# The gated tokens' product with wo: inside the recurrence's loop, or behind its last state

## The chip, the cores and the metric

The kernel runs on one core of a Trainium2 chip. The metric is the device time of one execution in microseconds (us). The kernel before took 2483.61 us (median of three runs, 2482.64 to 2483.89). One further execution was recorded by the hardware profiler; its trace is what this document reads.

Engines are named as in the profile: PE is TensorE's matmuls, PEld its weight loads, DVE is VectorE, ACT is ScalarE, POOL is GpSimd, SP is SyncE, which here only issues DMAs.

## The reference

The program is two layers over x of 32 sequences of 128 tokens, 512 wide. The first layer and the second layer's routed experts come earlier in the kernel and are not touched. The change lies in the last part, a recurrence over the 32 sequences followed by an output product:

```python
# z = r * y: the gated tokens, from the part before (32 x 128 x 512)
def step(c, xt):
    ft = sigmoid(xt @ wf.T + c @ uf.T + bf)
    it = sigmoid(xt @ wi.T + c @ ui.T + bi)
    gt = tanh(xt @ wc.T + c @ uc.T + bc)
    c = ft * c + it * gt
    return (c, None)
c_final, _ = lax.scan(step, c0, z)
h = tanh(einsum('tbi,oi->tbo', z, wo) + c_final @ uo.T + bo)
x = x1 + h
```

Two things matter. The steps of the scan depend on one another through the state c, which is 128 x 512. The product of z with wo does not depend on c at all; only the final sum does, which needs the last state.

## The kernel before

**Number format.** Every matmul with fp32 accuracy is made of three: both operands are split into a high and a low half (`split`, L64 on ACT for the high half, L65 on DVE for the low one), and `mm3` (L82) multiplies high by high, high by low and low by high for each of KD = 4 slices of the contraction. So one product of 128 x 512 by 512 x 512 is 12 matmuls of 512 columns. A weight pair takes 16 KB of each partition.

**Tiling.** A block b is one of NB = 32 steps of the scan (128 rows, one for each position in a sequence). Four blocks make a group: NG = 8 groups of GT = 512 rows. z of a group is held as `zs[g]`, a pair of halves in pool `zp`, which has two buffers.

**The loop** (from L1677 on) runs over t = 0 to 31. One step is, in the order of the program: three products of the state, `from_c` for c, i and f, each followed by its gate (`gate`: addition of the bias on DVE from PSUM, sigmoid or tanh on ACT); the new state (`new_c`, two DVE operations); the products of the next step's input, `from_x`, for c and i; four transposes of the new state (`turn`, tile ptC) and the split of the result, cT; `from_x` for f; then `gate_y` for block t+2. `gate_y` takes r through a sigmoid on ACT and multiplies it by y on DVE, transposes the product on PE (tile ptF, one PSUM bank) and splits it from PSUM into `zs[g]`. `get_y` then asks for r (a load on SP's queue) and y (an indirect gather on POOL's queue) two blocks ahead; both have two buffers.

The step ends with `unit(t - 2)`. A unit is one of 32 pieces of the product of z with wo: n is divided into the group g and the slice o of 128 output columns, and a unit is 12 matmuls into a PSUM bank poF. There are two banks for it (`ps_z`). For groups 0 to 4 ACT copies the result to `zo` and its own queue stores it to DRAM (`zo_d`); for groups 5 and 6 it stays on chip (`zok`); group 7's four results stay in PSUM. Groups are only complete once their fourth block is gated, so unit n is taken in step n + 2, and the last four (group 7) in steps 30 and 31 and behind them.

At t = 29 the input weights are no longer needed. Their memory (pool `wx_p`) is given to a pool `op`, and loads of stored results and of x1 begin (`load_groups`, `load_part`). Other pieces go into memory that other tiles leave free: the recurrent weights' pools `uci` and `uf_p`, the biases' tiles, staging tiles.

**Behind the last state**: `cu`, the product of the state with uo, 48 matmuls of 128 columns, into four PSUM banks; then `to_z`, which adds the same product, broadcast over the group's four blocks, to group 7's banks with 48 matmuls of 512 columns. Each of the 32 results then takes an addition of cu (DVE, L1768; not for group 7), a tanh with the bias bo1 (ACT, L1774), an addition of x1 on DVE and POOL by turns (L1777), and a store of 256 KB on SP's queue (L1778).

**Order.** The program's order gives the priority, but the framework places instructions for each engine ahead of time. Something that it expects to be ready can be placed ahead of something that is written earlier. At t = 31, 13 matmuls of units stand ahead of the transposes of the last state, though they are written behind them. [...]`issue_after` keeps a block of instructions behind a given one.

Of the kernel before, what the change touches and what calls it, by code (L numbers as in the profile page):

```python
# [20 lines left out]
P = 128  # L21
D = 512
KD = D // P
NB = 32
# [25 lines left out]
def tile_kernel(ctx: ExitStack, tc: tile.TileContext, a: dict, out: bass.AP):  # L50
# [40 lines left out]
    hid_d = [dram.tile([n, P, KD * P], F32, tag=f"hid{i}", name=f"hid_d{i}") for i, n in enumerate(PARTS)]  # L91
    xh_d = [dram.tile([n, P, KD * P], F32, tag=f"xh{i}", name=f"xh_d{i}") for i, n in enumerate(PARTS)]
    x1_d = dram.tile([NB, P, KD, P], F32, tag="x1", name="x1_d")
    zo_d = [dram.tile([P, KD, GT], F32, tag=f"zo{g}", name=f"zo_d{g}") for g in range(NG)]
    bias_d = dram.tile([E0 * P, 3 * KD], F32, tag="bias", name="bias_d")

    v_d = dram.tile([N, D], F32, tag="v", name="v_d")
# [1416 lines left out]

    with sf:
        kw = dict(reuse_waits="tile")
        ZS = 2

        zop = sf.enter_context(tc.tile_pool(name="zop", bufs=4, side="right", **kw))
        uf_p = sf.enter_context(tc.tile_pool(name="uf_p", bufs=1, side="right", **kw))  # L1520
# [33 lines left out]
        def gate_y(b):  # L1554
            g, j = divmod(b, GB)
            y, r = ys.pop(b)
            if b >= LEAD:
                nc.scalar.activation(r, r, AF.Sigmoid)
            nc.vector.tensor_tensor(r, y, r, ALU.mult)  # L1559
            if j == 0:  # L1560
                zs[g] = zp.tile([P, 2, KD, GT], FR, tag="z", name=f"z_{g}")
            pt = ps_y.tile([P, KD, P], F32, tag="t", name=f"ptF_{b}")
            for k in range(KD):
                nc.tensor.transpose(pt[:, k, :], r[:, bass.ts(k, P)], ident)  # L1564
            s = bass.ts(j, P)
            return split(zs[g][:, 0, :, s], zs[g][:, 1, :, s], pt)

        def turn(c, t):
            pt = ps_c.tile([P, KD, P], F32, tag="t", name=f"ptC_{t}")
# [29 lines left out]
            nc.vector.tensor_tensor(new, v["f"], v["i"], ALU.add)  # L1599
            return new  # L1600

        pos, zos, x1s = {}, {}, {}

        def unit(n, k0=0, k1=KD):

            if n < 0:
                return
            g, o = divmod(n, KD)
            last = g == NG - 1
            if k0 == 0:  # L1610
                pool, tag = ((ps_z, "z"), (ps_z, "z"), (ps_y, "t"), (ps_g, "g"))[o if last else 0]
                pos[o] = pool.tile([P, GT], F32, tag=tag, name=f"poF_{g}_{o}")
            po = pos[o]
            mm3(
                po, lambda h, k: wo1[:, h, k0 + k, bass.ts(o, P)],
                lambda h, k: zs[g][:, h, k0 + k, :], k1 - k0, k0 == 0, not last,
            )
            if last:
                pass
            elif g >= NG - 1 - ZS:  # L1620
                if o % 2 == 0:
                    zok = zop.tile([P, 2, GT], F32, tag="raw", name=f"zok_{g}_{o}")
                    zos[g, o], zos[g, o + 1] = zok[:, 0, :], zok[:, 1, :]
                nc.scalar.copy(zos[g, o], po)
            else:
                zo = yp.tile([P, GT], F32, tag="zo", name=f"zo_{g}_{o}")
                nc.scalar.copy(zo, po)
                nc.scalar.dma_start(out=zo_d[g][:, o, :], in_=zo)

        def load_groups(pool, tag, todo):  # L1630

            t = pool.tile([P, len(todo), KD, GT], F32, tag=tag, name="in_" + "_".join(f"{d}{g}" for d, g in todo))
            for n, (d, g) in enumerate(todo):
                if d == "x":
                    by = t[:, n].rearrange("p o q -> p (o q)").rearrange("p (b o q) -> p b o q", b=GB, q=P)
                    nc.sync.dma_start(
                        out=by.rearrange("p b o q -> p b (o q)"),
                        in_=x1_d[g * GB : (g + 1) * GB].rearrange("b p o q -> p b (o q)"),
                    )
                    for o in range(KD):  # L1640
                        x1s[g, o] = by[:, :, o, :]
                    continue
                nc.sync.dma_start(out=t[:, n], in_=zo_d[g])
                for o in range(KD):
                    zos[g, o] = t[:, n, o, :]

        def load_part(pool, tag, d, g, o, parts=1):
            t = pool.tile([P, parts, GT], F32, tag=tag, name=f"in_{d}{g}_{o}")
            if d == "x":
                for n in range(parts):  # L1650
                    x1s[g, o + n] = by = t[:, n, :].rearrange("p (b q) -> p b q", q=P)
                    nc.sync.dma_start(
                        out=by, in_=x1_d[g * GB : (g + 1) * GB, :, o + n, :].rearrange("b p q -> p b q")
                    )
                return
            nc.sync.dma_start(out=t, in_=zo_d[g][:, o : o + parts, :])
            for n in range(parts):
                zos[g, o + n] = t[:, n, :]

        ps, wx = {}, {}  # L1660

# [19 lines left out]
        for t in range(NB):  # L1681
            cT = cT_next
            v = {}
            if t == 0:
                done = from_x(0, ps, "ci", False, True)
                with tc.issue_after(done):
                    from_x(0, ps, "f", False, True)
                with tc.issue_after(z_done):
                    wo1 = weight("wo", keep_p, yp, 2, "zo", KD)
                for n in "cif":  # L1690
                    gate(t, n, ps, v, bias)
            elif t < NB - 1:
                for n in "cif":
                    late = from_c(t, n, ps, cT, False, True)
                    gate(t, n, ps, v, bias)
            else:
                for n in "cif":
                    from_c(t, n, ps, cT, True, True)
                    gate(t, n, ps, v, stash)
# [14 lines left out]
            for b in ((t + LEAD,) if t < NB - 4 else (NB - 2, NB - 1) if t == NB - 4 else ()):  # L1714
                gate_y(b)
                if b + LEAD < NB:
                    get_y(b + LEAD)
            for n in (t - 2,) if t < NB - 2 else (NB - 4, NB - 3) if t == NB - 2 else (NB - 2,):
                unit(n)
            if t == NB - 3:  # L1720
                sx.close()
                op = sf.enter_context(tc.tile_pool(name="op", bufs=1, side="right", **kw))
                load_groups(op, "a", [("x", 7), ("x", 6)])
                load_groups(op, "b", [("x", 5), ("x", 0)])
                load_groups(zp, "z", [("z", 0), ("x", 1)])
                uo1 = op.tile([P, 2, KD, D], FR, tag="uo", name="uo_hl")
                for k in range(KD):
                    raw = yp.tile([P, D], F32, tag="yr"[k % 2], name=f"raw_uo{k}")
                    nc.sync.dma_start(out=raw, in_=a["uo"][:, k, :])
                    split(uo1[:, 0, k], uo1[:, 1, k], raw)  # L1730
                with tc.issue_after(late):
                    load_part(first_p, "c0", "x", 3, 0)
                    load_part(first_p, "cT0", "x", 3, 1, 2)
                load_part(yp, "zo", "x", 3, 3)
                load_part(yp, "zo", "z", 2, 3)
            if t == NB - 2:
                for o, n in enumerate("cif"):
                    load_part(keep_p, "b" + n, "z", 2, o)
        load_groups(uci, "uc", [("z", 3), ("x", 4)])
        load_groups(uci, "ui", [("z", 4), ("z", 1)])  # L1740
        load_groups(uf_p, "uf", [("x", 2)])

        cT = cT_next
        unit(NB - 1, 0, KD // 2)
        cu = []
        for o in range(KD):
            pool, tag = (ps_c, "t") if o == 0 else (ps_g, "g")
            cu.append(pool.tile([P, P], F32, tag=tag, name=f"cu_{o}"))
            mm3(cu[o], lambda h, k: uo1[:, h, k, bass.ts(o, P)], lambda h, k: cT[:, h, k, :], KD)

        def to_z(o):
            mm3(
                pos[o], lambda h, k: uo1[:, h, k, bass.ts(o, P)],
                lambda h, k: cT[:, h, k, :].unsqueeze(1).to_broadcast([P, GB, P]), KD, False, True,
            )

        unit(NB - 1, KD // 2, KD)
        units = [(g, o) for g in (6, 5, 0, 1, 2, 3, 4) for o in range(KD)]
        for o in range(KD):
            units.insert(3 + 5 * o, (NG - 1, o))  # L1760
        for n, (g, o) in enumerate(units):
            if g == NG - 1:
                to_z(o)
                src = pos.pop(o)
                h = yp.tile([P, GT], F32, tag="y", name=f"hF_{g}_{o}")
            else:
                src = h = zos[g, o]
                nc.vector.tensor_tensor(  # L1768
                    h.rearrange("p (b t) -> p b t", t=P),
                    h.rearrange("p (b t) -> p b t", t=P),  # L1770
                    cu[o].unsqueeze(1).to_broadcast([P, GB, P]),
                    ALU.add,
                )
            nc.scalar.activation(h, src, AF.Tanh, bias=bo1[:, o : o + 1])  # L1774
            x1 = x1s[g, o]
            by = h.rearrange("p (b q) -> p b q", q=P)
            (nc.gpsimd if n % 2 else nc.vector).tensor_tensor(by, by, x1, ALU.add)  # L1777
            nc.sync.dma_start(out=out[g][:, o, :], in_=h)  # L1778


# [86 lines left out]
```

## Time and profile before

| | us |
|---|---|
| median of three runs | 2483.61 |
| the profiled execution's own time | 2483.24 |
| its span, first to last instruction | 2481.50 |
| first recurrent product (ps_c of t = 0) starts | 1796.07 |
| last matmul ends | 2459.82 |

| from 1796.07 to 2459.82 (663.75 us) | busy us |
|---|---|
| PE | 660.79 |
| DVE | 225.21 |
| ACT | 153.06 |
| POOL | 44.07 |

The trace gives each instruction's start and duration. Matmuls are pipelined, so a row of 12 shows a little more than twelve times their spacing; the spacing is read from the starts of successive rows. A name such as `poF<-z,wo_hl` is the tile that is written and those that are read. In a list of waits, the row names the engine and tile that waited, the one it waited for, the total in us, how often, and the longest. The granted clock is the share of TensorE's full clock that the chip allowed. In rows of DMAs, the last figure is the median time from issue to landing.

### The profile page before, as it was taken

What the parts mean: (1) busy time and instruction counts of PE and PEld (TensorE: products, weight loads), DVE (VectorE), ACT (ScalarE), POOL (GpSimd) and SP (SyncE); (2) the same over time, 40 slices, a digit from 0 to 9 for tenths busy, and PEclk for the clock granted to TensorE, in tenths of its full rate; (3) what the DMA queues carried; (4) which work ended last, traced back from release to release, by engine and by line L of the source; (5) the groups of instructions that cost most, each with busy time, mean ns of one, the idle gap of its engine ahead of it and who ended that gap; (6) DMA issues with size and microseconds to landing.
All of it is one profiled execution on the core that took longest, in us unless ns stands there. A gap on an engine that the chain in (4) does not pass through costs nothing.

```text
span 2481.5 us, 36586 instructions
## 1 busy us (share of the span) xinstructions
PE 2429.9 (98%) x12918; PEld 2057.4 (83%) x12918; DVE 1331.9 (54%) x2283; ACT 1035.4 (42%) x1826; POOL 410.5 (17%) x462
## 2 busy tenths in 40 slices
PE   8999999999999999999999999999999999999996
PEld 6788888888887888888888799999878888888885
DVE  8796654556567454365454586676643333333326
ACT  5545533443223644454554476666522222222214
POOL 1000022222232333322232100000010000000003
PEclk9999999999999999999999999999999999999998
DMA  6545555556564253342342577777431111111027
GB/s 211 150 126 175 187 172 165 187 183 228 172 211 149 95 160 114 103 154 69 104 161 87 189 262 236 227 222 231 166 110 39 42 40 43 43 39 39 26 72 280
DMA packets 193404, 351.63 MB, mean 142 GB/s; under 512 B 37504, under 2 KB 72368, under 8 KB 190144
## 3 DMA queue, kind: packets, MB, share of 16 engines
q1 hardware_dynamic: 141792, 245.99, 29.9%
q0 software_dynamic: 36448, 75.95, 10.3%
q10 hardware_dynamic: 14976, 27.27, 3.0%
q8 instruction: 108, 1.77, 0.3%
q14 instruction: 80, 0.66, 0.1%
HBM read 373.94 MB, written 88.65 MB: 186 GB/s over the span
## 4 chain that ended last, share of the span: by engine, by line
PE 52%; DVE 1%; DMA 1%; ACT 0%; issue 0%; POOL 0%; POOLq 0%; DVEq 0%; ACTq 0%
PE phD L82 7%; PE ps_c L82 7%; PE ps_f L82 7%; PE ps_i L82 7%; PE poD L82 7%; PE poF L82 3%; PE po L82 3%; PE pb L82 2%; PE pv L82 2%; PE ptF L1564 1%; PE ptC L1571 1%; PE ptD L1431 1%; PE ptB L1256 0%; PE pr L1176 0%; DMA rowsD<-xk_d,slot_t 0%
## 5 line engine op out<-in xcount | busy, mean ns | idle before, releaser
L65 DVE TENSOR_TENSOR wD<-rawD,wD 128x1024 fp32r<-128x1024 f32 x128 | 156.5, 1229 | 82.1 <-ACT wD L64 82.1
L82 PE MATMUL p<-xhl,swu 128*128 128x512 f32 x768 | 190.4, 399 | 6.2 <-ACT xhl L64 6.2
L82 PE MATMUL p<-xhl,kept_u 128*128 128x512 f32 x768 | 185.9, 397 | 0.7 <-DVE kept_u L65 0.7
L82 PEld LDWEIGHTS phD<-xe,wD 128*128 128x128 f32 x1536 | 184.3, 189 | 2.1 <-ACT xe L64 0.9
L82 PE MATMUL phD<-xe,wD 128*128 128x256 f32 x1536 | 185.0, 280 | 0.7 <-ACT xe L64 0.7
L82 PE MATMUL poD<-wD,hD 128*128 128x512 f32 x768 | 181.6, 392 | 0.0
L82 PEld LDWEIGHTS p<-xhl,swu 128*128 128x128 f32 x768 | 145.7, 192 | 36.8 <-ACT xhl L64 6.2
L82 PEld LDWEIGHTS p<-xhl,kept_u 128*128 128x128 f32 x768 | 143.0, 189 | 30.4 <-DVE kept_u L65 1.1
L82 PEld LDWEIGHTS poD<-wD,hD 128*128 128x128 f32 x768 | 141.9, 188 | 28.3
L64 ACT CAST wD<-rawD 128x1024 fp32r<-128x1024 f32 x128 | 133.3, 1046 | 56.1 <-PE poD L82 54.1
L290 POOL DMA_INDIRECT xg<-in_x_rows_dram,blk_t x71 | 67.7, 954 | 442.6 <-PE ptx L300 242.9
L1536 POOL DMA_INDIRECT y<-res_d,gat_i x32 | 30.5, 952 | 573.8 <-DVE r L1559 492.9
L82 PE MATMUL pur<-r,xb 128*128 x792 | 110.3, 288 | 3.2 <-issue 1.2
L82 PE MATMUL por<-r,hbr 128*128 x396 | 107.9, 407 | 1.2 <-ACT hbr L64 1.1
L65 DVE TENSOR_TENSOR xb<-ptx,xb 128x512 fp32r<-128x512 f32 x68 | 47.0, 691 | 105.7 <-ACT xb L64 103.9
L82 PEld LDWEIGHTS pur<-r,xb 128*128 128x128 f32 x792 | 98.3, 189 | 5.3 <-issue 1.8
L82 PE MATMUL poF<-z,wo_hl 128*128 128x512 f32 x384 | 96.4, 399 | 0.0
L82 PE MATMUL ps_f<-wf_hl,z 128*128 128x512 f32 x384 | 96.2, 399 | 0.0
L82 PE MATMUL pb<-rT,Wo_hl 128*128 128x256 f32 x768 | 95.2, 281 | 0.3 <-DVE rT L65 0.2
L82 PE MATMUL ps_c<-wc_hl,z 128*128 128x512 f32 x384 | 94.7, 396 | 0.7 <-ACT z L64 0.7
L82 PE MATMUL pv<-w_recept_hl,xr 128*128 128x512 f32 x384 | 94.2, 395 | 0.0
L82 PE MATMUL acc<-swd,as 128*128 128x512 f32 x384 | 93.5, 390 | 0.0
(1031 smaller groups left out, 4950.1 us busy)
## 6 DMA issues: line engine op xcount, KB each, us to landing
rawD<-in_w_key_dram SPq DMA_DIRECT2D x64, 512.0 KB, 4.2
rawD<-in_w_value_dram SPq DMA_DIRECT2D x64, 512.0 KB, 4.2
swr<-in_sw_dram SPq DMA_DIRECT2D x120, 256.0 KB, 3.3
o_d<-obr SPq DMA_DIRECT2D x66, 256.0 KB, 2.3
rraw<-in_rw_dram SPq DMA_DIRECT2D x32, 256.0 KB, 3.0
xc<-in_x_dram SPq DMA_DIRECT2D x32, 256.0 KB, 3.6
hid_d<-o ACTq DMA_DIRECT2D x32, 256.0 KB, 2.3
xh_d<-xc SPq DMA_DIRECT2D x32, 256.0 KB, 2.9
```

What stands on the lines that cost most here:

```text
L64: first = nc.scalar.copy(hi, src).ins
L65: done = nc.vector.tensor_tensor(lo, src, hi.bitcast(F32), ALU.subtract).ins
L82: done = nc.tensor.matmul(ps, lhsT=left(hl, k), rhs=right(hr, k), start=start and k + n == 0, stop=stop and 3 * k + n == last,)
L290: nc.gpsimd.indirect_dma_start(out=xg[i], out_offset=None, in_=a["x_rows"], in_offset=bass.IndirectOffsetOnAxis(ap=blk_t[:, i : i + 1], ax ...
L1431: nc.tensor.transpose(pt[:, k, :], xe[:, s, bass.ts(k, P)], ident)
L1536: got = nc.gpsimd.indirect_dma_start(out=y, out_offset=None, in_=res_d, in_offset=bass.IndirectOffsetOnAxis(ap=gat_i[:, b : b + 1], axis=0),)
L1564: nc.tensor.transpose(pt[:, k, :], r[:, bass.ts(k, P)], ident)
L1571: nc.tensor.transpose(pt[:, k, :], c[:, bass.ts(k, P)], ident)
```

## The change

1. `gate_y` copies the transposed block from PSUM to SBUF on ACT (`zt`) for groups 0 to 5 and splits from there; the copy is also stored, on SP's queue, to a new array `z_d`. Groups 6 and 7 (`ON_CHIP = 2`) stay as halves on chip, and are split from PSUM as before.
2. The loop has no unit up to t = 29. Group 6's four units stand where group 7's stood: two at t = 30, one at t = 31, one behind the loop. Their results are copied to SBUF (`put_by`).
3. wo is loaded and split at t = 4 through the `zop` tiles in two pieces of 512 KB, instead of at t = 0 in four of 256 KB.
4. `zo_d`, `load_groups` and `load_part` go. At t = 29 the pool `op` takes two buffers for z of a group (`fetch_z`), two for x1 of a group (`fetch_x1`), each 1 MB, and uo.
5. `cu` is copied to SBUF by ACT, with the bias added there. `to_z` goes.
6. Behind the state the groups run in the order 6, 7, 0, 1, 2, 3, 4, 5. For each: the split of a z three groups ahead in that order (into memory of `zp` and of the recurrent weights), the fetch of another z, the four units (none for group 6) into the four PSUM banks of `ps_g`, each followed by its result (addition of cu, tanh, addition of x1, store), and the fetch of x1 for the group after next.

```diff
-            return split(zs[g][:, 0, :, s], zs[g][:, 1, :, s], pt)
+            src = pt
+            if g < NG - ON_CHIP:
+                src = yp.tile([P, KD, P], F32, tag="zo", name=f"zt_{b}")
+                nc.scalar.copy(src, pt)
+                nc.sync.dma_start(out=z_d[g][j], in_=src)
+            return split(zs[g][:, 0, :, s], zs[g][:, 1, :, s], src)
...
+        def unit(g, o):
+
+            pos[g, o] = po = ps_g.tile([P, GT], F32, tag="g", name=f"poF_{g}_{o}")
+            mm3(po, lambda h, k: wo1[:, h, k, bass.ts(o, P)], lambda h, k: zs[g][:, h, k, :], KD)
+
+        def put_by(g, o):
+            if o % 2 == 0:
+                zw = zop.tile([P, 2, GT], F32, tag="raw", name=f"zw_{g}_{o}")
+                zws[g, o], zws[g, o + 1] = zw[:, 0, :], zw[:, 1, :]
+            nc.scalar.copy(zws[g, o], pos.pop((g, o)))
+
+        def fetch_z(g):
+            zr[g] = op.tile([P, GB, KD, P], F32, tag="zr", bufs=2, name=f"zr_{g}")
+            nc.sync.dma_start(
+                out=zr[g].rearrange("p b k q -> p b (k q)"), in_=z_d[g].rearrange("b p k q -> p b (k q)")
             )
...
+        def fetch_x1(g):
+            x1s[g] = op.tile([P, GB, KD, P], F32, tag="x1", bufs=2, name=f"x1F_{g}")
...
+        def split_z(g, pool, tag):
+            raw = zr.pop(g)
+            zs[g] = pool.tile([P, 2, KD, GT], FR, tag=tag, name=f"zF_{g}")
+            for k in range(KD):
+                hi, lo = (zs[g][:, h, k, :].rearrange("p (b q) -> p b q", q=P) for h in range(2))
+                split(hi, lo, raw[:, :, k, :])
...
-                with tc.issue_after(z_done):
-                    wo1 = weight("wo", keep_p, yp, 2, "zo", KD)
...
-            for n in (t - 2,) if t < NB - 2 else (NB - 4, NB - 3) if t == NB - 2 else (NB - 2,):
-                unit(n)
+            if t == 4:
+                with tc.issue_after(last_r[0]):
+                    wo1 = weight("wo", keep_p, zop, 4)
+            for o in {NB - 2: (0, 1), NB - 1: (2,)}.get(t, ()):
+                unit(NG - 2, o)
+                put_by(NG - 2, o)
...
+                for g in range(2):
+                    fetch_z(g)
                 uo1 = op.tile([P, 2, KD, D], FR, tag="uo", name="uo_hl")
...
+                for g in (NG - 2, NG - 1):
+                    fetch_x1(g)
         cT = cT_next
-        unit(NB - 1, 0, KD // 2)
-        cu = []
+        unit(NG - 2, 3)
+        put_by(NG - 2, 3)
+
+        cu = gp.tile([P, KD, P], F32, tag="vc", name="cu")
         for o in range(KD):
-            pool, tag = (ps_c, "t") if o == 0 else (ps_g, "g")
-            cu.append(pool.tile([P, P], F32, tag=tag, name=f"cu_{o}"))
-            mm3(cu[o], lambda h, k: uo1[:, h, k, bass.ts(o, P)], lambda h, k: cT[:, h, k, :], KD)
-
-        def to_z(o):
-            mm3(
-                pos[o], lambda h, k: uo1[:, h, k, bass.ts(o, P)],
-                lambda h, k: cT[:, h, k, :].unsqueeze(1).to_broadcast([P, GB, P]), KD, False, True,
+            pc = ps_c.tile([P, P], F32, tag="t", name=f"cu_{o}") if o % 2 else ps_y.tile([P, P], F32, tag="t", name=f"cu_{o}")
+            mm3(pc, lambda h, k: uo1[:, h, k, bass.ts(o, P)], lambda h, k: cT[:, h, k, :], KD)
+            nc.scalar.activation(cu[:, o, :], pc, AF.Identity, bias=bo1[:, o : o + 1])
+
+        def result(g, o, n):
+            src = zws.pop((g, o)) if (g, o) in zws else pos.pop((g, o))
+            h = yp.tile([P, GB, P], F32, tag="yr"[n % 2], name=f"hF_{g}_{o}")
+            nc.vector.tensor_tensor(
+                h, src.rearrange("p (b t) -> p b t", t=P), cu[:, o, :].unsqueeze(1).to_broadcast([P, GB, P]), ALU.add
             )
...
+            nc.scalar.activation(h, h, AF.Tanh)
+            (nc.gpsimd if n % 2 else nc.vector).tensor_tensor(h, h, x1s[g][:, :, o, :], ALU.add)
+            nc.sync.dma_start(out=out[g][:, o, :], in_=h.rearrange("p b t -> p (b t)"))
+
+        order = [NG - 2, NG - 1, *range(NG - 2)]
+        homes = [(zp, "z"), (uci, "uc"), (uci, "ui"), (uf_p, "uf"), (zp, "z"), (uci, "uc")]
+        split_z(0, *homes[0])
+        for m, g in enumerate(order):
+            if m + 1 < NG - 2:
+                split_z(m + 1, *homes[m + 1])
+            if m + 2 < NG - 2:
+                fetch_z(m + 2)
+            for o in range(KD):
+                if g != NG - 2:
+                    unit(g, o)
+                result(g, o, m * KD + o)
+            if m + 2 < NG:
+                fetch_x1(order[m + 2])
```

More of the change, by code (lines that the diff above doesn't have):

```diff
@@ L93, in tile_kernel @@
     x1_d = dram.tile([NB, P, KD, P], F32, tag="x1", name="x1_d")
-    zo_d = [dram.tile([P, KD, GT], F32, tag=f"zo{g}", name=f"zo_d{g}") for g in range(NG)]
+    z_d = [dram.tile([GB, P, KD, P], F32, tag=f"z{g}", name=f"z_d{g}") for g in range(NG)]
     bias_d = dram.tile([E0 * P, 3 * KD], F32, tag="bias", name="bias_d")
@@ L1516, in tile_kernel @@
         kw = dict(reuse_waits="tile")
-        ZS = 2
+        ON_CHIP = 2
         zop = sf.enter_context(tc.tile_pool(name="zop", bufs=4, side="right", **kw))
@@ L1600, in new_c @@
             return new
[L1602 to L1613, printed above, removed]
-            mm3(
-                po, lambda h, k: wo1[:, h, k0 + k, bass.ts(o, P)],
-                lambda h, k: zs[g][:, h, k0 + k, :], k1 - k0, k0 == 0, not last,
-            )
[L1618 to L1658, printed above, removed]
+        pos, zr, x1s, zws = {}, {}, {}, {}
@@ new lines, in fetch_x1 @@
+        def fetch_x1(g):
+            x1s[g] = op.tile([P, GB, KD, P], F32, tag="x1", bufs=2, name=f"x1F_{g}")
+            nc.sync.dma_start(
+                out=x1s[g].rearrange("p b k q -> p b (k q)"),
+                in_=x1_d[g * GB : (g + 1) * GB].rearrange("b p k q -> p b (k q)"),
+            )
+        def split_z(g, pool, tag):
[4 more added lines that the diff above has]
+                split(hi, lo, raw[:, :, k, :])
@@ L1722, in tile_kernel @@
                 op = sf.enter_context(tc.tile_pool(name="op", bufs=1, side="right", **kw))
-                load_groups(op, "a", [("x", 7), ("x", 6)])
-                load_groups(op, "b", [("x", 5), ("x", 0)])
-                load_groups(zp, "z", [("z", 0), ("x", 1)])
+                for g in range(2):
+                    fetch_z(g)
                 uo1 = op.tile([P, 2, KD, D], FR, tag="uo", name="uo_hl")
@@ L1730, in tile_kernel @@
                     split(uo1[:, 0, k], uo1[:, 1, k], raw)
[L1731 to L1739, printed above, removed]
@@ L1740, in tile_kernel @@
-        load_groups(uci, "ui", [("z", 4), ("z", 1)])
-        load_groups(uf_p, "uf", [("x", 2)])
+                for g in (NG - 2, NG - 1):
+                    fetch_x1(g)
         cT = cT_next
-        unit(NB - 1, 0, KD // 2)
-        cu = []
+        unit(NG - 2, 3)
+        put_by(NG - 2, 3)
+        cu = gp.tile([P, KD, P], F32, tag="vc", name="cu")
         for o in range(KD):
-            pool, tag = (ps_c, "t") if o == 0 else (ps_g, "g")
-            cu.append(pool.tile([P, P], F32, tag=tag, name=f"cu_{o}"))
-            mm3(cu[o], lambda h, k: uo1[:, h, k, bass.ts(o, P)], lambda h, k: cT[:, h, k, :], KD)
@@ L1751, in to_z @@
-        def to_z(o):
-            mm3(
-                pos[o], lambda h, k: uo1[:, h, k, bass.ts(o, P)],
-                lambda h, k: cT[:, h, k, :].unsqueeze(1).to_broadcast([P, GB, P]), KD, False, True,
-            )
[L1757 to L1778, printed above, removed]
```

## The prediction

> **What bounds the kernel now.** I read the groups by engine first, then TensorE's timeline over the recurrence, then busy time by stretches, then the waits and the end. The page's first row says where to look:
>
> ```profile
> PE 2429.9 (98%) x12918; PEld 2057.4 (83%) x12918; DVE 1331.9 (54%) x2283; ACT 1035.4 (42%) x1826; POOL 410.5 (17%) x462
> ```
>
> A share of 98% is an average, so the question is whether TensorE waits in the stretch that is rebuilt. Its timeline (start, duration, instruction, count) shows the last step without a product with wo and the beginning of the next, which has one:
>
> ```profile
> 1845.74 3.01 PE L82 MATMUL ps_c<-uc_hl,cT 128*128 128x512 f32 x12
> 1848.59 2.88 PE L82 MATMUL ps_i<-ui_hl,cT 128*128 128x512 f32 x12
> 1851.31 2.88 PE L82 MATMUL ps_f<-uf_hl,cT 128*128 128x512 f32 x12
> 1854.03 2.88 PE L82 MATMUL ps_c<-wc_hl,z 128*128 128x512 f32 x12
> 1856.75 2.89 PE L82 MATMUL ps_i<-wi_hl,z 128*128 128x512 f32 x12
> 1859.47 0.60 PE L1571 MATMUL ptC<-ident,c 128*128 128x128 f32 x4
> 1859.83 3.02 PE L82 MATMUL ps_f<-wf_hl,z 128*128 128x512 f32 x12
> 1862.68 0.60 PE L1564 MATMUL ptF<-ident,r 128*128 128x128 f32 x4
> 1863.04 3.01 PE L82 MATMUL poF<-z,wo_hl 128*128 128x512 f32 x12
> 1865.88 2.88 PE L82 MATMUL ps_c<-uc_hl,cT 128*128 128x512 f32 x12
> ```
>
> Twelve matmuls come every 2.72 us (1848.59 to 1851.31): 0.2267 us each. The reader should see that a step without wo (1845.74 to 1863.04, 17.30 us) is as gapless as one with it. Busy time by stretches (length, then PE, PEld, DVE, ACT, POOL with counts, granted clock, DMA share, GB/s) says the same, and shows two other states:
>
> ```profile
> 1808.00:1812.00 4.00, 4.00 (x12) 3.22 (x13) 1.49 (x3) 1.40 (x2) 2.71 (x4) 0.50 0.97 345
> ...
> 1845.74:1863.04 17.30, 17.30 (x84) 14.30 (x82) 6.13 (x9) 3.71 (x6) 0.94 (x1) 1.00 0.11 30
> ...
> 2105.80:2125.80 20.00, 20.00 (x93) 16.55 (x92) 6.23 (x9) 4.17 (x7) 0.95 (x1) 1.00 0.13 41
> ```
>
> PE is full both times, DVE and ACT a third or less. The first row follows the loop's only waits of TensorE:
>
> ```profile
> PE ptF L1564 <- DVE r L1559: 2.1, 1, 2.1
> PE ps_c L82 <- ACT z L64: 0.7, 1, 0.7
> ```
>
> After them the clock was 0.50. So the recurrence is bound by TensorE's matmuls, and moving matmuls is worth nothing by itself. The end is different:
>
> ```profile
> 2448.76 11.06 PE L82 MATMUL poF<-cT,uo_hl 128*128 128x512 f32 x48
> ...
> 2474.45 1.26 POOL L1777 TENSOR_TENSOR in_z_z<-in_z_z,in_z_x 128x512 f32<-128x512 f32 x1 [0.91 <-ACT in_z_z L1774]
> ```
>
> TensorE ends at 2459.82 and the span at 2481.50: 21.68 us in which it does nothing while DVE (14.5 us busy), POOL (13.8) and ACT (8.8) work off 32 results.
>
> **The change, part by part.** All sums are against the profiled execution: 2483.24 us, with a span of 2481.50 and 1.74 around it. It lies 0.37 us below the median of the runs, 2483.61.
>
> **Removed: the state's product added group by group.** `to_z` put cT·uo into the four accumulators of group 7, 48 matmuls of 512 columns. Now every group takes the small `cu`, which costs its 48 narrow matmuls as before. The row gives 48 x 0.2267 = 10.9 us, all on TensorE with nothing beside it to hide behind: **-10.9**. The Trainium skill ("TensorE: Matmul & The Clock Gate", Back-to-back issue gap) gives a sustained 131 ns for 512 columns, by which these 48 were worth 6.3 us. The trace's spacing of 227 ns holds for every wide matmul here, so I take 10.9.
>
> **Moved: the products with wo.** 28 units of 12 matmuls leave the steps up to t = 29 (28 x 2.72 = 76.2 us). Group 6's four stand at t = 30, 31 and behind it, where group 7's units covered the gates. 28 units stand behind the state: 28 x 2.72 = 76.2. TensorE's sum: **0**. What matters is whether PE stays full on both sides.
>
> *In the loop* the cover of the gates must hold without wo. At t = 1 f's product ends at 1854.19, the new c is done at 1857.04 (VectorE row 1856.35, 0.69 us) and its transposes run at 1859.47: 2.4 us early. cT's low half is done at 1861.47 and first wanted at 1863.04: 1.6 us early. New beside it, per step: a copy of ptF on ACT (0.57, like the zo copy that goes) ahead of z's cast, and a store of z on SP ahead of the next load of r. The load then goes out some 1.0 us later (copy 0.57 plus one 0.33 us issue). Behind it in the queues stand r's sigmoid (0.63), r·y (0.69) and POOL's gather of y; behind those on ACT and DVE, gate c. Gate c may be 1 to 2 us late, but gate i, 2.7 us behind it, and then f wait for TensorE anyway; r itself is wanted a step later. The z copy stands behind cT's cast by ptF's place. Cost **0**; if all of the z and r work stood ahead of cT it would be 3.2 us against 1.6 of slack.
>
> *wo's loading* moves from t = 0 to t = 4: two casts of 1.05 on ACT, two subtractions of 1.27 on DVE, against 2.4 us of slack: 0, at most 1 once. *The first gate* has no cover: TensorE waits for its z (the 0.7 row), and the copy comes ahead: **+0.6** (0 to 2, as the clock is low there). *At t = 28* two transposes share one PSUM bank, and wo matmuls stood between: **+0.4** (0 to 0.7: one copy).
>
> *Behind the state* T is the end of cu. Each group asks TensorE for 48 x 0.2267 = 10.9 us. ACT: 4 casts of 0.55 (uo's: 2.19 for four) and 4 tanh of 0.71 = 5.0. DVE: 4 subtractions of 0.62, 4 additions of 0.68, 2 of 0.7 to 1.2 = 6.6 to 7.6. POOL: 2 of 1.3 to 1.6. DMA: z 1 MB, x1 1 MB, out 1 MB = 3.1 MB in 10.9 us = 290 GB/s, against 352 that the trace moved from 2410 to 2430. So TensorE is the longest, with results four PSUM banks (8.2 us) deep. z's splits stand three groups ahead of their use. x1 is fetched some 3 us after group m and wanted 15 us after it, for m+2; a load of that size took:
>
> ```profile
> in_x_x<-x_d SPq DMA_DIRECT2D x4, 1024.0 KB, 8.2
> ```
>
> 8.2 us median, 14.0 for the slowest kind: covered. The tight place is the first pass: group 6 has no products there, so the fetches of z2, z3 and x1 of group 0 go out within some 4 us of T, with two groups' output. z2's split is written ahead of group 7's results. The same page of the skill (Architectural detail) calls ACT and DVE strict FIFOs; by that rule those results wait for z2. With z2 issued at about T and 8.2 us, the first result goes at T+9 to T+11, and the first unit of group 0 needs its bank at T+10.9: between 0 and some 6 us of wait. The PE row is against a literal order: 13 wo matmuls ran ahead of ptC at t = 31, so what is ready is placed first. I take **0**; bounds 0 and 14.
>
> **The end.** Behind the last matmul now come one result, 0.68 + 0.71 + 1.4 (POOL; 1.26 to 1.6) with 0.2 of handoffs, and the 5.79 us from the last addition (2475.71) to the end of the span: 8.8 instead of 21.7: **-12.9**. The other 31 results hide under matmuls; x1 and out move as many bytes as before.
>
> Sum: 2483.24 - 10.9 - 12.9 + 0.6 + 0.4 = 2460.4; plus 0.37 for the median: **2460.8 us**.
>
> **The rivals.** *Starved tail.* The fetches of the first pass (5.2 MB of z2, z3, x1 and two outputs) take 15 us at 352 GB/s, so z2 or x1 may land late. With z2 at T+15, its split and a result behind it, TensorE resumes at T+17 instead of T+10.9: +6; after a gap like the one at 1804 the clock was 0.50 for some 4 us, +2: 2469. A second such stop in the next pass: 2475. For it: the FIFO order, and one 14 us load. Against: the depth of four banks.
>
> *Slower: the chain of c loses its cover.* One mechanism: with wo gone, only f's input product and ptF (3.2 us) lie between ptC and the next recurrent product. If the copy, cast and subtraction of z and r's sigmoid and product were placed ahead of cT's cast and subtraction, cT would be 3.2 us later, 1.6 past the slack: 28 x 1.6 = 45, 2505 us. It decides from 22.8 / 28 = 0.8 us a step. For it: the slack is only 1.6. Against: t = 0 and 1 run without wo and without a gap.
>
> *The end stays long.* If DVE, ACT and POOL fall four results behind, 8.2 us come back: 2469. Against: 7.6 of 10.9 us per group.
>
> **How the numbers follow.** Forecast 60%, starved tail 20%, long end 7%, lost cover 11%, start or end shifts beyond these 2%. Runs spread by 1.2 us in 2484; 0.2% (5 us) is what a measurement tells from no change. Faster is the forecast, both middle rivals and a little of the rest: 0.87; same, a tail that stops three times: 0.04; slower, lost cover above 0.8 a step: 0.09. The range runs from 2456 (an end and a start some 4 us shorter) to 2475 (two stops in the tail): it leaves out lost cover and the far tail.
>
> **What would show it.** Steps of 17.3 us with TensorE gapless from t = 1 to 29; 48 fewer wide matmuls; TensorE ending some 9 us before the span, not 22; granted clock 1.00 to the last unit. Wrong if ps_c waits for cT, if a stretch behind cu shows PE below full or the clock below 1.00, or if the last results run far behind the last unit.

## The result, and the profile after

The changed kernel took 2463.62 us (median of four runs, 2458.60 to 2465.97); the kernel before, beside it, 2483.12. The ratio is 0.992, with a 95% interval of 0.9903 to 0.9937. The profiled execution took 2462.88 us with a span of 2461.1. The forecast was 2460.8.

The first row of the page shows 48 matmuls fewer and the same share:

```profile
PE 2421.7 (98%) x12870; PEld 2048.8 (83%) x12870; DVE 1349.3 (55%) x2309; ACT 1051.4 (43%) x1852; POOL 408.9 (17%) x462
```

TensorE's timeline (start, duration, instruction, count) shows the step t = 3, one of those that had a product with wo before:

```profile
1862.94 3.01 PE L82 MATMUL ps_c<-uc_hl,cT 128*128 128x512 f32 x12
...
1876.67 0.60 PE L1578 MATMUL ptC<-ident,c 128*128 128x128 f32 x4
1877.02 3.02 PE L82 MATMUL ps_f<-wf_hl,z 128*128 128x512 f32 x12
1879.88 0.60 PE L1566 MATMUL ptF<-ident,r 128*128 128x128 f32 x4
1880.23 3.01 PE L82 MATMUL ps_c<-uc_hl,cT 128*128 128x512 f32 x12
```

From one ps_c to the next 17.29 us pass, without a gap. The list of TensorE's waits from 1790 us on says that it stays so for the rest of the recurrence, and that a wait has come behind it:

```profile
PE ptF L1566 <- DVE r L1561: 1.7, 2, 1.2
PE ps_c L82 <- ACT z L64: 1.4, 1, 1.4
PE cu L82 <- ACT cu L1724: 0.6, 1, 0.6
```

The first two rows lie at the start of the loop, as the two rows before did. The third is new. The timeline of the end, TensorE alone:

```profile
2366.78 2.79 PE L82 MATMUL cu<-cT,uo_hl 128*128 128x128 f32 x24
2370.14 5.16 PE L82 MATMUL cu<-cT,uo_hl 128*128 128x128 f32 x24 [0.56 <-ACT cu L1724]
2375.10 12.12 PE L82 MATMUL poF<-z,wo_hl 128*128 128x512 f32 x48
2387.06 65.44 PE L82 MATMUL poF<-zF,wo_hl 128*128 128x512 f32 x288
```

The 288 matmuls of groups 0 to 5 run through at 0.227 us each: no load, split or result holds them up. But the second half of cu took 5.16 us where the first took 2.79, and the next 48 wide matmuls 1.1 us more than the 11.06 that 48 took before. The stretches show why (length, then PE, PEld, DVE, ACT, POOL, granted clock, DMA share, GB/s):

```profile
2366.80:2369.00 2.20, 2.20 (x22) 2.20 (x20) 2.13 (x5) 2.20 (x5) 0.00 (x0) 1.00 0.00 0
2369.00:2371.00 2.00, 1.44 (x11) 1.29 (x10) 2.00 (x4) 1.09 (x3) 0.00 (x0) 0.85 0.57 208
2371.00:2373.00 2.00, 2.00 (x12) 2.00 (x11) 1.30 (x3) 0.89 (x2) 0.00 (x0) 0.50 1.05 368
...
2377.00:2380.00 3.00, 3.00 (x14) 2.50 (x13) 2.90 (x5) 1.31 (x3) 0.00 (x0) 0.96 0.47 64
...
2440.00:2452.50 12.50, 12.50 (x56) 10.02 (x54) 4.85 (x7) 2.83 (x5) 2.58 (x2) 1.00 0.29 108
2452.50:2461.10 8.60, 0.00 (x1) 0.00 (x0) 0.69 (x1) 0.63 (x1) 1.26 (x1) 0.69 0.16 61
```

These shares put the clock at half from about 2370.4 to 2377.2, 6.8 us. The last row is the end: 8.6 us behind the last matmul, with one result in them, where it was 21.7. What the third product of cu waited for stands in ACT's queue:

```profile
2367.64 2.17 ACT L64 CAST zF<-zr 128x512 fp32r<-128x512 f32 x4
2369.73 0.36 ACT L1724 ACTIVATE cu<-cu,bo_sb 128x128 f32<-128x128 f32 x1
```

cu has two PSUM banks. The first product was done at about 2368.2 (12 of the 24 matmuls that took 2.79 us), but ACT copied it out at 2369.73, behind four casts of a z. No product with such a z (zF) began before 2387.06.

### The profile page after: what moved, and what is told of

It is laid out like the page before. It is cut to its first block, busy times and chain, and to the rows that moved or that the text cites. A ratio compares the mean times of both kernels' runs of the same rounds, so it can differ in the third digit from the quotient of the medians.

```text
span 2461.1 us, 36619 instructions
## 1 busy us (share of the span) xinstructions
PE 2421.7 (98%) x12870; PEld 2048.8 (83%) x12870; DVE 1349.3 (55%) x2309; ACT 1051.4 (43%) x1852; POOL 408.9 (17%) x462
## 4 chain that ended last, share of the span: by engine, by line
PE 49%; issue 2%; DMA 1%; POOL 1%; DVE 1%; ACT 1%; POOLq 0%; DVEq 0%; ACTq 0%
PE phD L82 7%; PE ps_c L82 7%; PE ps_f L82 7%; PE ps_i L82 7%; PE poD L82 7%; PE po L82 3%; PE pb L82 2%; PE pv L82 2%; POOL hF L1733 1%; PE ptC L1578 1%; PE ptD L1431 1%; PE ptF L1566 1%; PE poF L82 0%; PE ptB L1256 0%; DMA rowsD<-xk_d,slot_t 0%
## 5 line engine op out<-in xcount | busy, mean ns | idle before, releaser
L82 PE MATMUL ps_c<-uc_hl,cT 128*128 128x512 f32 x384 | 96.2, 399 | 0.0
L815 POOL DMA_INDIRECT o<-o_d,s_i x64 | 66.7, 1042 | 172.3 <-PE pth L835 84.4
```

The costliest lines, as they stand in the source:

```text
L82: done = nc.tensor.matmul(ps, lhsT=left(hl, k), rhs=right(hr, k), start=start and k + n == 0, stop=stop and 3 * k + n == last,)
L815: nc.gpsimd.indirect_dma_start(out=o[n], out_offset=None, in_=o_d, in_offset=bass.IndirectOffsetOnAxis(ap=idx[:, b : b + 1], axis=0),)
```

## The experiments

Times are medians, with the ratio to the kernel before measured beside it. "Recurrence on" is the part of the profiled span from the first ps_c to the end; the parts ahead of it, whose instructions the change leaves alone, took between 1795.7 and 1801.4 us in the profiles and blur the medians. The runs of the kernel before itself lay 7.6, 11.0 and 7.4 us apart in the three sets of runs beside these experiments, where the forecast had counted on 1.2. So differences of a few us are read from the stretches of the profiles.

| | median us | ratio, 95% interval | recurrence on, us |
|---|---|---|---|
| before | 2483.12 to 2486.00 | | 685.4 |
| changed | 2463.62 | 0.992, 0.9903 to 0.9937 | 665.4 |
| changed, again | 2463.56 | 0.9907, 0.9891 to 0.9924 | 664.9 |
| cu in four banks | 2459.81 | 0.9892, 0.9875 to 0.9908 | 662.3 |
| cu between units | 2464.72 | 0.9907, 0.9890 to 0.9923 | 662.9 |
| 48 matmuls put back | 2475.30 | 0.9963, 0.9949 to 0.9976 | 676.7 |
| before, without the 48 | 2487.23 | 1.0007, 0.9998 to 1.0017 | 687.6 |
| changed, f's product first | 2478.12 | 0.9965, 0.9952 to 0.9979 | 678.3 |
| before, f's product first | 2482.66 | 0.9988, 0.9978 to 0.9998 | 682.1 |
| four banks, last addition on DVE | 2459.21 | 0.9896, 0.9879 to 0.9913 | 659.3 |
| the same, again | 2458.69 | 0.9880, 0.9861 to 0.9899 | 659.5 |
| changed, last addition on DVE | 2461.60 | 0.9900, 0.9886 to 0.9915 | 665.0 |

**The changed kernel again**, to learn its spread.

> The changed kernel, unaltered. Theory A (a wait of 0.56 us in the products of cu, because ACT copies cu out of a bank late, lets the clock fall to half for some 6 us, and how long depends on when it comes): the runs lie apart by some 7 us, 2458 to 2466, and each run's mean granted clock goes with its time, 0.001 of the clock for about 2.5 us. Rival B (the spread is that of any kernel here): runs within 3 us of one another, as before's are, and no such order of clock and time.

The runs lay between 2462.83 and 2464.56, no wider apart than before's, which lay between 2481.50 and 2489.10 beside them: theory A's account of the spread falls, though within these 1.7 us the slowest run had the lowest clock (0.994) and the fastest the highest (0.996). The wait and the slow stretch were there again (two waits of 0.48 and 0.67 us, then half clock for 3.4 us). The 7 us between the first four runs stay unexplained; the start of the recurrence, which lay up to 5.7 us apart in the profiles, could make most of them.

**cu in four banks.**

```diff
-            pc = ps_c.tile([P, P], F32, tag="t", name=f"cu_{o}") if o % 2 else ps_y.tile([P, P], F32, tag="t", name=f"cu_{o}")
+            pool, tag = ((ps_y, "t"), (ps_c, "t"), (ps_z, "z"), (ps_z, "z"))[o]
+            pc = pool.tile([P, P], F32, tag=tag, name=f"cu_{o}")
```

> The four products of cu go to four PSUM banks (two of them idle in the changed kernel) instead of two, so none waits for ACT to copy one out. Theory A: no wait in the stretch of cu, clock 1.00 through it, 3.8 us less than the changed kernel's profiled run: about 2459, with runs within 3 us. Rival B (48 narrow matmuls in a row let the clock fall by themselves): the 0.56 us go, the clock still falls to 0.50: about 2462. Rival C (the cost was not on the path): unchanged, 2463.

Theory A's number: 2459.81, 3.75 less than the changed kernel measured beside it (2463.56); the slowest of these runs, 2460.61, lies below the fastest of those, 2462.83. The timeline and the stretches of its end:

```profile
2368.05 5.47 PE L82 MATMUL cu<-cT,uo_hl 128*128 128x128 f32 x48
2373.36 11.15 PE L82 MATMUL poF<-z,wo_hl 128*128 128x512 f32 x48
2384.36 65.44 PE L82 MATMUL poF<-zF,wo_hl 128*128 128x512 f32 x288
```

```profile
2368.05:2373.36 5.31, 5.31 (x49) 5.30 (x48) 4.61 (x9) 3.97 (x9) 0.00 (x0) 1.00 0.42 152
```

From the start of cu to the first unit of group 0 it is 16.31 us, against 20.28. ACT is as late as before (its first copy of cu starts 2.85 us behind cu's start); it only holds nobody up. The 48 narrow matmuls in a row keep a clock of 1.00, which rules out B. It is the same in all profiles of the changed kernel and its variants. The five in which cu waited (0.56 us, or two waits of about 0.5 and 0.7) show half clock from there on, for 3.4 or 6.8 us. The four in which it did not wait (four banks three times, and the next experiment) show 1.00.

**cu between the units of group 7.**

```diff
             nc.scalar.activation(cu[:, o, :], pc, AF.Identity, bias=bo1[:, o : o + 1])
+            unit(NG - 1, o)
...
-                if g != NG - 2:
+                if g < NG - 2:
```

> Group 7's four units stand between the four products of cu, so that narrow and wide matmuls alternate and ACT has 2.7 us for each copy out of a bank; cu keeps its two banks. Theory A: no wait, clock 1.00, about 2459. Rival B (narrow matmuls in a row): also about 2459, since no more than 12 narrow ones follow one another. With the four banks, this tells A from B: if only this one is at 2459, it is B.

The median missed the expected 2459 and says no gain. The profile says that the end is mended:

```profile
2373.60:2390.08 16.48, 16.48 (x98) 14.37 (x96) 11.84 (x18) 8.68 (x18) 1.28 (x1) 1.00 0.71 243
```

The same stretch, cu and group 7, takes 16.48 us at full clock. In this execution the recurrence began at 1801.4 instead of 1795.7, behind instructions that are the same in both kernels. From there on it is 662.9 us, like the four banks. So this run agrees with A in its profile, while its median alone would have told nothing. Whether a late start also lengthened its other runs (2460.84 to 2465.66) is not shown.

**The 48 matmuls put back**, their result unused:

```diff
+        for o in range(KD):
+            pd = ps_z.tile([P, GT], F32, tag="z", name=f"extra_{o}")
+            mm3(
+                pd, lambda h, k: uo1[:, h, k, bass.ts(o, P)],
+                lambda h, k: cT[:, h, k, :].unsqueeze(1).to_broadcast([P, GB, P]), KD,
+            )
```

> The changed kernel with the 48 wide matmuls of cT and uo put back behind cu, into two idle PSUM banks; nothing reads their result. The prediction's sum (TensorE is the end's bound, and each wide matmul costs 0.2267 us): 10.9 us more than the changed kernel, 2474.5. Rival (the end is bound by loads or by DVE's results, and matmuls are hidden): less than 3 us more, under 2467.

2475.30, 11.7 more than the changed kernel. TensorE at the end:

```profile
2375.52 13.34 PE L82 MATMUL extra<-cT,uo_hl 128*128 128x512 f32 x48
2388.69 11.04 PE L82 MATMUL poF<-z,wo_hl 128*128 128x512 f32 x48
2399.57 65.44 PE L82 MATMUL poF<-zF,wo_hl 128*128 128x512 f32 x288
```

From the start of cu (2367.66) to the first unit of group 0 it is 31.91 us, against 20.28: 11.6 more, of which 10.9 are the 48 matmuls at full clock. The other 0.7 goes with cu's waits, two here (0.47 and 0.67) where there was one of 0.56. In the changed kernel the end is TensorE's, and each matmul there costs its time.

**The kernel before without them.**

```diff
-                lambda h, k: zs[g][:, h, k0 + k, :], k1 - k0, k0 == 0, not last,
+                lambda h, k: zs[g][:, h, k0 + k, :], k1 - k0, k0 == 0, k1 == KD,
...
-                to_z(o)
-                src = pos.pop(o)
                 h = yp.tile([P, GT], F32, tag="y", name=f"hF_{g}_{o}")
+                nc.scalar.copy(h, pos.pop(o))
             else:
-                src = h = zos[g, o]
-                nc.vector.tensor_tensor(
-                    h.rearrange("p (b t) -> p b t", t=P),
-                    h.rearrange("p (b t) -> p b t", t=P),
-                    cu[o].unsqueeze(1).to_broadcast([P, GB, P]),
-                    ALU.add,
-                )
-            nc.scalar.activation(h, src, AF.Tanh, bias=bo1[:, o : o + 1])
+                h = zos[g, o]
+            nc.vector.tensor_tensor(
+                h.rearrange("p (b t) -> p b t", t=P),
+                h.rearrange("p (b t) -> p b t", t=P),
+                cu[o].unsqueeze(1).to_broadcast([P, GB, P]),
+                ALU.add,
+            )
+            nc.scalar.activation(h, h, AF.Tanh, bias=bo1[:, o : o + 1])
```

> The kernel before, without the 48 wide matmuls of cT and uo: group 7's four results get cu by an addition on DVE like the others (behind a copy out of PSUM on ACT). The prediction's sum counts these matmuls as 10.9 us of their own: 2484.4 - 10.9 = 2473.5. Rival (in the kernel before they ran beside 32 results that DVE, POOL and ACT work off until 2475.7, so they cost nothing there, and the whole gain of the change is that the results are covered): within 3 us of before, rather slower, since DVE gets four additions of 0.68 more.

The rival is right: 1.0007, nothing gained. TensorE's last matmul and the stretches behind it, in this kernel:

```profile
2448.63 1.61 PE L82 MATMUL poF<-z,wo_hl 128*128 128x512 f32 x6
```

```profile
2450.00:2460.00 10.00, 0.23 (x1) 0.00 (x0) 10.00 (x15) 6.73 (x12) 5.30 (x5) 0.70 0.72 258
2460.00:2470.00 10.00, 0.00 (x0) 0.00 (x0) 10.00 (x16) 6.51 (x10) 7.25 (x6) 0.50 0.69 241
```

TensorE stops at 2450, and DVE is full for 20 us and more. From the start of cu (2442.98) to the end of the span it is 41.9 us, against 39.8 in the kernel before: about what four more additions on DVE take (2.7). The kernel before shows the same engine busy from the first product of cu on, and full in the stretch of the 48 matmuls (last two rows):

```profile
2443.00:2476.00 33.00, 16.82 (x95) 14.32 (x93) 30.57 (x44) 20.78 (x32) 24.48 (x16) 0.79 0.79 287
...
2450.00:2455.00 5.00, 5.00 (x24) 4.14 (x23) 5.00 (x8) 2.68 (x4) 3.22 (x3) 1.00 0.89 322
2455.00:2459.80 4.80, 4.80 (x22) 3.66 (x20) 4.80 (x9) 4.66 (x8) 3.94 (x3) 1.00 0.79 280
```

So the end before was DVE's queue, the additions of the 32 results, and the 48 matmuls ran beside it at no cost.

**f's product ahead of the transposes**, in both kernels, to see how thick the cover of the recurrence is:

```diff
             if t < NB - 2:
                 from_x(t + 1, ps, "ci", True, False)
-            cT_next = turn(c, t + 1)
             if t < NB - 2:
                 from_x(t + 1, ps, "f", True, False)
+            cT_next = turn(c, t + 1)
```

> The changed kernel with f's input product (2.72 us) ahead of the state's transposes instead of behind them, so that only ptF's transposes (0.36) lie between ptC and the next product of the state. If the cover without wo is as thin as the trace says (cT's high half 0.65 us behind ptC, its low half 1.4), TensorE waits 0.3 to 1.0 us in each of 29 steps: 9 to 29 us more than the changed kernel, 2472 to 2492. Rival (the cover was ample): 2463.6.

> The same exchange in the kernel before, where a product with wo (2.72 us) still stands behind the transposes from t = 2 on: no wait but in the first two steps, 2484 to 2486. Rival (the exchange costs something else): as much more as in the changed kernel.

The changed kernel loses 14.6 us, the kernel before nothing (2482.66 beside 2486.00, an interval that ends just below 1). One step of the changed kernel with this edit, and the sum of the waits:

```profile
2114.07 0.60 PE L1578 MATMUL ptC<-ident,c 128*128 128x128 f32 x4
2114.51 0.60 PE L1566 MATMUL ptF<-ident,r 128*128 128x128 f32 x4
2115.35 0.73 PE L82 MATMUL ps_c<-uc_hl,cT 128*128 128x512 f32 x2 [0.24 <-ACT cT L64]
...
2131.83 0.60 PE L1578 MATMUL ptC<-ident,c 128*128 128x128 f32 x4
```

```profile
PE ps_c L82 <- ACT cT L64: 7.2, 29, 0.3
```

A step is 17.76 us instead of 17.29: 0.24 of it is the wait, the other 0.23 lies between the shorter runs of matmuls around it. In the kernel before, wo's product fills the same place:

```profile
2100.76 0.60 PE L1564 MATMUL ptF<-ident,r 128*128 128x128 f32 x4
2101.12 2.98 PE L82 MATMUL poF<-z,wo_hl 128*128 128x512 f32 x12
2103.94 2.88 PE L82 MATMUL ps_c<-uc_hl,cT 128*128 128x512 f32 x12
```

So wo's product was a second cover behind f's. Taking it alone costs nothing; taking both costs half a us in each step.

**The last addition on DVE.** With four banks, and alone:

```diff
-            (nc.gpsimd if n % 2 else nc.vector).tensor_tensor(h, h, x1s[g][:, :, o, :], ALU.add)
+            (nc.vector if n % 2 else nc.gpsimd).tensor_tensor(h, h, x1s[g][:, :, o, :], ALU.add)
```

> The changed kernel with cu in four banks and the additions of x1 exchanged, so that the last of the 32 is DVE's (0.69 us) and not POOL's (1.26): 0.6 us less than with four banks alone, 2459.2. Rival (POOL's additions now delay something earlier): 2459.8 or more.

> Four banks for cu and the exchange of the x1 additions, once more. In its first profile the end of the span came 3.8 us after the last addition (DVE's), where the changed kernel and the one with four banks alone have 5.8 after POOL's. If that belongs to the engine of the last addition, it is 3.8 again, and TensorE's end lies 5.9 us before the span's, not 8.6. If it was chance, 5.8 and about 8.0.

> The changed kernel with only the exchange of the x1 additions (the last is DVE's); cu keeps its two banks. If the end belongs to the engine of the last addition: 5.9 us from the last matmul to the end of the span, and 2.7 less than the changed kernel, about 2460.9. If only the addition's own time counts: 8.0, and 2463. The wait in cu and the half clock behind it stay, 3.8 us, whatever the end does.

The medians with four banks, 2459.21 and 2458.69, can't be told from 2459.81 for the four banks alone. In the profiles the last matmul ends 5.9 us before the span in all three executions with DVE last, and 8.6 in the changed kernel and with four banks alone. So that part of the expectation came, and all medians with four banks lie below those of both kernels. With two banks the wait in cu stayed, as expected. The median of 2461.60 is 2.0 less than the changed kernel's, but its ratio, 0.99, can't be told from 0.9907, and from the recurrence on the profile is 665.0 us, no less than the changed kernel's 664.9 to 665.4: the 2.7 us gained at the end were lost ahead of it (a wait of 0.88 us at t = 5, a longer first gate, and 20.95 us from the start of cu to group 0).

## Why the prediction was right, and where it was not

The time lay 2.8 us above the forecast, inside the range, and the forecast's case is the one that came. In the profiled executions the sum was 2460.4 and the measurement 2462.9. Step by step:

- **The loop, cost 0:** shown. Steps of 17.29 us, no wait from t = 1 on. (The step from 1845.74 in the kernel before, which the forecast calls t = 1, is t = 2: unit 0 stands at its end.) Lost cover, the rival on the slower side, did not come. The exchange of f's product shows that TensorE does wait when the cover is thinner; the order of work that this rival assumed, z's and r's ahead of cT's, was not tried.
- **wo's load, "0, at most 1 once":** 0 in the profiled execution of the result. In four of seven other profiles with the same loop the transposes at t = 5 waited once, 0.3 to 0.9 us, for a state that DVE made late behind wo's subtractions.
- **The first gate, +0.6:** about +0.35. From the first recurrent product to f's first input product it is 20.92 us, where it was 20.57. All nine profiles with the changed start show 20.5 to 21.5, the three with the start of before 18.2 to 20.6, so the gate does cost something, within the forecast's 0 to 2. That both products begin at nearly the same time (1816.62 and 1816.64) is luck: the recurrence began 0.37 us earlier.
- **t = 28, +0.4:** 0. Seven matmuls of the next recurrent product were placed between the two transposes, as units were before.
- **TensorE behind the state:** no starved tail and no long end. z, x1 and the splits held up no matmul behind cu, though one result did wait 3.2 us for the store of an earlier one; the four banks of the units covered that.
- **The end, 8.8 us:** 8.6.
- **cu, "costs its 48 narrow matmuls as before":** this step failed. It was priced at 0 as work that stays, and the copy out of PSUM that is new with it was not followed through ACT's queue. With two banks, and casts of z ahead of the copy, TensorE waited 0.56 us, and its clock stood at half for 6.8 us from there on: 3.75 us by the medians with four banks, 3.97 by the stretch from cu to group 0. The forecast looked for such a wait in the results of the first pass, one stage too late. A clock below 1.00 behind cu stood among its signs of being wrong, and that sign came.
- **"-10.9, all on TensorE with nothing beside it to hide behind":** the number fits a sum made along TensorE, but it is no saving of its own. DVE was full beside those matmuls (9.80 of the 9.80 us from 2450 on), where the forecast looked at DVE only behind the last matmul. The kernel before without them is no faster, and the changed kernel with them is 11.7 us slower. The gain is one thing, not two: the results used to begin behind the last state and keep DVE busy for some 31 us, and now they lie under matmuls that have to be done anyway. Only because TensorE became the bound of the end did leaving out the 48 matmuls count.

Against the sum for the profiled execution the miss is 2.5 us, and the differences make it up. From the start of cu to the last matmul it took 85.7 us. The forecast's terms make 82.1 of the kernel before there (18.1, less 10.9, and 330 matmuls more at 0.2267). That is 3.7 more. The recurrence began 0.4 earlier, the first gate and t = 28 cost 0.25 and 0.4 less than forecast, the end 0.2 less. So the forecast is closer than its step on cu deserved: small terms on the other side, and an early start that is chance, took back a third of it.

## What to carry to other kernels

Work of a bound engine that does not depend on a serial loop is worth most as cover for what can only begin behind the loop; before moving it out, check with the loop's own steps that something else still covers the recurrence. A saving that is read off one engine's path holds only while that engine is the bound: in the stretch at the end, ask first which engine is full. And where a product is newly copied out of PSUM, follow the copying engine's queue from the moment the bank is full, since a short wait of TensorE can cost several times its length.

## What was unexpected

- A wait of 0.56 us within narrow matmuls was followed by 6.8 us at half clock. The narrow matmuls alone did not do that (5.3 us at 1.00), nor did 29 waits of about 0.24 us between transposes and wide matmuls (clock 1.00 from 1830 to 2300), nor single waits that were longer: 0.84 and 0.88 us ahead of the transposes at t = 5, among wide matmuls, in the runs with cu between units and with the last addition on DVE alone (1.00 through it and for 10 us behind it), and 1.45 us at t = 0 in the kernel before without the 48. At the loop's start, where two or three waits lie close together (2.07 and 0.68 us in the kernel before), the clock fell to half too. So a single wait as short as 0.56 us brought it down only within narrow matmuls; no experiment varied the two one by one. The Trainium skill ("TensorE: Matmul & The Clock Gate", HAM oscillation) gives as a rule of thumb no idle gaps above about 3.4 us; here much less was enough.
- From the end of the last addition to the end of the span it was 5.8 us with POOL last and 3.8 with DVE last, in three profiles of three with DVE last. In both the last store's transfer is over within about 2 us. What the other 2 us are, no run shows.
